# Expert tiles 7 to 17 of a GAT and mixture-of-experts kernel: rows loaded as 32 by 32 blocks and turned by VectorE

## The chip, the core and the metric

The kernel runs on one core of a Trainium2 chip. The metric is the device time of one launch in microseconds; lower is better. The engines are TensorE (PE, with its weight loads shown apart as PEld), VectorE (DVE), ScalarE (ACT), GpSimd (POOL) and SyncE (SP, which here only issues DMAs).

## What is computed

One layer has two halves. The first is a graph attention over 4096 nodes of 256 features with 4 heads of 64 and a dense 4096 by 4096 adjacency matrix. The second is a mixture of 8 experts with hidden size 1024, of which every node uses two.

```python
def _L0_ffn_ref(x, Wg, bg, W1, b1, W2, b2):
    xf = x.reshape(-1, D)
    gate_logits = xf @ Wg + bg
    top_w, top_i = jax.lax.top_k(gate_logits, TOP_K)
    top_w = jax.nn.softmax(top_w, axis=-1)
    w_dense = jnp.sum(jax.nn.one_hot(top_i, E, dtype=xf.dtype) * top_w[..., None], axis=1)
    out = jnp.zeros_like(xf)
    for e in range(E):
        h = jax.nn.gelu(xf @ W1[e] + b1[e], approximate=False)
        out = out + w_dense[:, e:e + 1] * (h @ W2[e] + b2[e])
    return out.reshape(B, L, D)

x = x + _L0_gnn_ref(_layernorm(x, axis=-1), adj, ...)
x = x + _L0_ffn_ref((_layernorm(x, axis=-1))[None], ...)[0]
```

All of it is in float32. The change touches the second half only.

## The kernel before

**The attention half** walks over the rows of the result in four blocks of 1024 and, for each, over 32 tiles of 128 neighbours. VectorE makes the weights of a tile (L1686), TensorE sums rows and denominators with them (L1195, L1204). While a block of rows is summed, the block before it is finished, normalised and routed: each row's two experts are found, and POOL writes the row (256 values and four numbers: two weights, the row's number and its first expert) to both experts' lists in HBM with indirect DMAs (L1382, tensor `lists`). So the lists fill block by block.

**The expert half** begins at about 778 us of the profile. It goes over tiles of an expert's list, in an order that is written out in `todo`: nine tiles `early` and eight tiles `mid`, each of 256 rows that are known to be full once the first three blocks have been routed; then eight tiles `final`, one for the rest of each list, of 288 to 512 rows (`FINAL`); then two tiles `rest` of 256 rows. Counted from 0, tiles 0 to 16 are the seventeen full ones. The first tile's rows and its first weights are loaded while the attention still runs. The last block of rows is finished and routed in pieces (`between`) beside tiles 0 to 5.

For each tile i the loop at the end of `forward` does, in this order of the program:

- `fetch` of tile i+1, all DMAs of SP's one queue: the expert's second bias (`b2b`, L1786), its first weights (`w1`, 1 MB, issued in `load_first`, L597) and its second weights (`w2`, 1 MB, L1793). `w1`, `w2` and `b2b` have two buffers each, so `w1` of a tile waits until TensorE has done the first product of two tiles before, `w2` until it has done the second, and `b2b` until ScalarE has scaled it (`b2s`, L1889).
- `up`: the first product, `ph`, 32 matmuls of 256 columns for a full tile (L1867), with a gelu by ScalarE of each of the eight results (L1871).
- `turn` of tile i+1: `prepare` makes the bias, the row numbers and the shares on VectorE (L1805 to L1835), and then the rows, which the experts' products need with features on partitions, are turned.
- `down`: the second product, `po`, again 32 matmuls of 256 columns for a full tile (L1901), in two halves of 128 rows. VectorE scales each half into `o` (L1914, nine buffers), and POOL adds it to the output with an indirect DMA (L1926).

On TensorE the order of a tile is thus up(i), the transposes of tile i+1, down(i). That order is kept by `queue` and `order_of` while the last block is being routed.

**Rows are loaded and turned in two ways.** For the seventeen full tiles `load_rows_of` (L554) loads 256 rows of 1040 bytes with one DMA into a buffer `early` (`ROOM` = 10 buffers): ten tiles ahead of the loop, and one more in each turn of the loop until all are loaded. `turn_rows_of` (L600) then transposes them on TensorE, 2 x 2 squares of 128 by 128 against the identity (L604), and ScalarE (L606) or VectorE (L608) copies the two results from PSUM to `xT`. For `final` and `rest` tiles `load_blocks_of` (L575) issues nine DMAs: one for the four numbers of each row (`known`, L580) and eight (two halves of the features by four quarters of the partitions, L587), each of which puts runs of 32 floats so that every 32 by 32 block stands where its transpose has to be. One VectorE instruction turns all blocks (`nc.vector.transpose`, L1851). `xr`, `known` and `xT` have two buffers each.

Loads of tiles behind the tenth (`late`) wait only for list entries that the third block wrote, not for those of the last block; loads of `final` and `rest` tiles wait for all of them, and for POOL's writes of zeros behind the lists' ends (L507).

Each SP DMA uses the next of eight completion semaphores, and before SP issues one it waits until the DMA eight places before it has landed.

Of the kernel before, what the change touches and what calls it, by code (L numbers as in the profile page):

```python
# [10 lines left out]
F32 = mybir.dt.float32  # L11
# [18 lines left out]
CH = P  # L30
TT = 2 * CH
WT = 4 * CH
FINAL = (16, 15, 15, 15, 13, 13, 12, 9)
LIST = 36 * CH
# [10 lines left out]
def gat_then_moe(  # L45
# [19 lines left out]
    nc = tc.nc  # L65
    N, D = x.shape
    H, _, K = W.shape
    E, _, F = W1.shape
# [10 lines left out]
    EARLY, BOTH = (-(-(2 * (N - k * R) - E * (TT - 1)) // TT) for k in (2, 1))  # L79
    MID = BOTH - EARLY  # L80
    LATE = 2 * N // TT - BOTH
    SURE = 2
    ROOM = 10
    KT = -(-N // TT)
    LAG = 6

# [1 line left out]
    W_1, W_2, ID, FIRST, RW = D, D + 1, D + 2, D + 3, D + 4  # L88
# [18 lines left out]
    lists = nc.dram_tensor("lists", [E * LIST, RW], F32, kind="Internal").ap()  # L107
# [111 lines left out]
    def forward(apart, stack):  # L219
# [49 lines left out]
        def tables(tag, width):  # L269

            return {
                "expert": moe_tile(f"expert{tag}", [P, width]),
                "mark": moe_tile(f"mark{tag}", [P, width]),
                "own": moe_tile(f"own{tag}", [P, width, E]),
                "place": moe_tile(f"place{tag}", [P, width]),
                "rows": moe_tile(f"rows{tag}", [P, width]),
                "float": moe_tile(f"float{tag}", [P, 2, width]),
                "int": moe_tile(f"int{tag}", [P, 2, width], I32),
                "past": moe_tile(f"past{tag}", [P, width, E]),
                "upto": moe_tile(f"upto{tag}", [P, E]),  # L280
            }
# [61 lines left out]
        early, mid, rest, final, over = tables("e", EARLY), {}, {}, {}, {}  # L343
# [174 lines left out]
        listed, earlier = [], []  # L518

        def after(ins, other, reason):  # L520
            tc.add_manual_dep(
                ins, other.name,
                mybir.DependencyInfo(mybir.DependencyClass.Sync, mybir.DependencyReason.DATA),
                reason=reason,
            )
# [25 lines left out]
        def entry(t, row, i, top):  # L551
            return nc.values_load(
                t["int"][0:1, row, i : i + 1], engines=[mybir.EngineType.SP],
                min_val=0, max_val=top, skip_runtime_bounds_check_because=why,  # L554
            )

        def load_rows_of(t, i, xr, late=False):
            rows = TT
            first = entry(t, 1, i, E * LIST - WT)
            ins = nc.sync.dma_start(  # L560
                xr, lists[bass.ds(first, rows), :].rearrange("(c p) d -> p c d", p=CH)
            ).ins
            if late:
                for i in earlier:
                    after(ins, i, "rows of the tile")
                for i in listed + clearing:
                    tc.declare_no_dep(ins, i.name, reason="rows behind those of the tile")
            else:
                for i in listed:
                    after(ins, i, "rows of the tile")  # L570

        def rows_of_job(t, i):
            return FINAL[i] * Q if t is final else TT

        def load_blocks_of(t, i, xb, known):  # L575


            first = entry(t, 1, i, E * LIST - WT)
            n = known.shape[1] * CH
            begun = [nc.sync.dma_start(  # L580
                known, lists[bass.ds(first, n), D:].rearrange("(c p) d -> p c d", p=CH)
            )]
            rows = lists[bass.ds(first, rows_of_job(t, i)), :]
            for c in range(DC):
                for a in range(P // Q):
                    here = c * P + a * Q
                    begun.append(nc.sync.dma_start(  # L587
                        xb[ts(a, Q), c], rows[:, here : here + Q].rearrange("(k p) d -> p k d", p=Q)
                    ))
            for ins in begun:  # L590
                for i in listed:
                    after(ins.ins, i, "rows of the tile")

        def load_first(t, i, w1):

            e = entry(t, 0, i, E - 1)
            nc.sync.dma_start(w1, W1[bass.ds(e, 1)].rearrange("o (c p) f -> p (o c) f", p=P))  # L597


        def turn_rows_of(xr, xT):  # L600
            for c in range(DC):
                pt = bank([P, TT], "pt")
                for k in range(TT // CH):
                    order_of(nc.tensor.transpose(pt[:, ts(k, CH)], xr[:, k, ts(c, P)], ident))  # L604
                if c % 2 == 0 or strict[0] or (ordered[0] and given_out):
                    nc.scalar.copy(xT[:, c, :], pt)  # L606
                else:
                    nc.vector.tensor_copy(xT[:, c, :], pt)  # L608
# [3 lines left out]
        with ExitStack() as layer:  # L612
# [964 lines left out]
            def first_tile():  # L1577

                load_rows_of(early, 0, xr0)
                load_first(early, 0, w10)  # L1580
# [26 lines left out]
            if not apart:  # L1607

                with tc.tile_pool(name="gen", bufs=2) as work:
# [12 lines left out]
                    for b in range(NB):  # L1622
                        mine = range(b * B, (b + 1) * B)
                        rows, top = er0[:, 0], er0[:, 1]
# [136 lines left out]
        work = ffn.enter_context(tc.tile_pool(name="ffn", bufs=2))  # L1761

        full_rows = [xr0]
# [9 lines left out]
        def fetch(t, i):  # L1773

            rows = rows_of_job(t, i)
            nch = -(-rows // CH)
            if t is early or t is mid:
                xr = full_rows[i + EARLY * (t is mid)]
                known = xr[:, :, D:]
            else:  # L1780
                xr = work.tile([P, DC, rows // Q, Q], F32, tag="xr", name="xr")
                known = work.tile([CH, nch, RW - D], F32, tag="known", name="known")
                load_blocks_of(t, i, xr, known)
            e = entry(t, 0, i, E - 1)
            b2b = work.tile([CH, D], F32, tag="b2b", name="b2b")
            nc.sync.dma_start(b2b, b2[bass.ds(e, 1)].to_broadcast([CH, D]))  # L1786
            if t is early and i == 0:
                w1 = w10
            else:
                w1 = work.tile([P, DC, F], F32, tag="w1", name="w1")  # L1790
                load_first(t, i, w1)
            w2 = work.tile([P, FC, D], F32, tag="w2", name="w2")
            nc.sync.dma_start(w2, W2[bass.ds(e, 1)].rearrange("o (c p) d -> p (o c) d", p=P))  # L1793
            job = {"t": t, "i": i, "xr": xr, "known": known, "w1": w1, "w2": w2, "nch": nch, "b2b": b2b}
            job["rows"] = rows
            job["last"] = t is rest and i == SURE - 1

            job["into"] = out[: N - R] if t is early or t is mid else out
            return job
# [38 lines left out]
        def turn(job):  # L1838
            xr = job["xr"]
            if given_out:  # L1840
                with tc.issue_after(given_out[-1]):
                    prepare(job)
            else:
                prepare(job)
            if job["t"] is early and job["i"] == 0:
                return xT0
            xT = work.tile([P, DC, job["rows"]], F32, tag="xT", name="xT")
            if job["t"] is early or job["t"] is mid:
                turn_rows_of(xr, xT)
            else:  # L1850
                nc.vector.transpose(  # L1851
                    xT.rearrange("p c i -> p (c i)"), xr.rearrange("p c k q -> p (c k q)")
                )
            return xT
# [134 lines left out]
        given = []  # L1989

        def load_full(i):
            xr = work.tile([CH, 2, RW], F32, tag="early", name="early", bufs=ROOM)
            load_rows_of(*((early, i) if i < EARLY else (mid, i - EARLY)), xr, i > ROOM)
            full_rows.append(xr)

        for i in range(1, ROOM + 1):
            load_full(i)
            if i in (1, 4):
                jobs.append(fetch(*todo[len(jobs)]))
            if i in (1, 2):  # L2000
                given.append(loads_of(b0 + i - 1, (residuals, large)[i - 1]))
        job = jobs[0]
        xT = turn(job)
        for i in range(len(todo)):
            if i + 1 == len(jobs) and i + 1 < len(todo):
                jobs.append(fetch(*todo[i + 1]))
            nxt = jobs[i + 1] if i + 1 < len(todo) else None
            if i and len(full_rows) < BOTH:
                load_full(len(full_rows))
            hT = up(job, xT)  # L2010
            between(2 * i)
            if nxt:
                xT = turn(nxt)
            giving = down(job, hT)
            next(giving)
            if nxt:
                next(giving, None)
            between(2 * i + 1)
            if tails:
                tails.pop(0)()  # L2020
            job = nxt
# [84 lines left out]
```

## Time and profile before

| what | value |
|---|---|
| median of 3 runs (1264.42 to 1270.94) | 1264.79 us |
| the profiled execution's own time | 1259.9 us |
| its span, first to last instruction | 1258.2 us |
| mean granted TensorE clock | 0.997 |
| PE / DVE / ACT / POOL busy | 1243.7 / 842.8 / 451.6 / 240.2 us |
| PE matmul of a tile's first product (L1867) | 864 of them, mean 423 ns |
| PE transposes of expert tiles (L604) | 68 of 128x128, median 273 ns |
| VectorE transposes of 128x512 (L1851) | 2, mean 711 ns |
| SP row loads (early<-lists) | 16 of 260 KB |
| SP block loads (xr<-lists) of 256 rows | 16 of 32 KB |

Busy times are sums of an engine's instruction records. Matmuls are pipelined: a record lasts longer than the distance from one matmul to the next, so the path is read from the chain of waits, which gives start, length and number of instructions of each piece. Window views give for a stretch of the span the length, then the busy time and number of instructions of PE, PEld, DVE, ACT and POOL, then the granted clock, the mean busy share of the 16 DMA engines (it can pass 1 in a short window) and the GB/s. A timeline row gives start, length, engine, line and operation; a bracket gives the idle time before it and what ended that.

### The profile page before, as it was taken

The numbers are of one execution on the slowest core, as the hardware profiler recorded it, in microseconds if no ns is written. First come the engines' busy times: TensorE is split into PE (matmuls) and PEld (weight loads), VectorE is DVE, ScalarE is ACT, GpSimd is POOL, SyncE is SP. The second block draws the span as 40 slices with busy tenths as digits, with TensorE's granted clock in tenths as the row PEclk, the third lists the DMA queues.
The fourth block names the chain that finished last, engine by engine and source line by source line (L and its number), as shares of the span: only waits on it lengthen the run. The fifth ranks groups of instructions, "written<-read, shape, count | busy, mean of one in ns | idle before, by whom it ended". The sixth has DMA issues, their size and how long they took to land.

```text
span 1258.2 us, 22490 instructions
## 1 busy us (share of the span) xinstructions
PE 1243.7 (99%) x8916; PEld 650.9 (52%) x8916; DVE 842.8 (67%) x1566; ACT 451.6 (36%) x929; POOL 240.2 (19%) x217
## 2 busy tenths in 40 slices
PE   9999999999999999999999999999999999999997
PEld 5444444332232332332325324888888876666686
DVE  7998887879999989999999996845111121111120
ACT  4332322255522375322655322533333332222322
POOL 4000000001002601006110024135222322122222
PEclk9999999999999999999999999999999999999999
DMA  6333433436533656335366423967777795454662
GB/s 215 118 119 124 158 105 102 166 102 133 187 105 104 231 118 201 103 100 158 112 167 194 119 80 108 329 184 225 234 208 222 207 210 115 102 139 105 139 156 42
DMA packets 131603, 190.22 MB, mean 151 GB/s; under 512 B 45560, under 2 KB 101744, under 8 KB 131104
## 3 DMA queue, kind: packets, MB, share of 16 engines
q1 hardware_dynamic: 109456, 145.39, 38.7%
q0 software_dynamic: 20544, 36.74, 13.2%
q10 hardware_dynamic: 1488, 6.55, 1.4%
q8 instruction: 72, 1.18, 0.4%
q14 instruction: 43, 0.35, 0.1%
HBM read 155.77 MB, written 29.74 MB: 147 GB/s over the span
## 4 chain that ended last, share of the span: by engine, by line
PE 94%; DVE 3%; issue 1%; DMA 1%; ACT 1%; POOLq 0%; SPq 0%; DVEq 0%; ACTq 0%
PE acc L1195 33%; PE po L1901 18%; PE ph L1867 17%; PE den L1204 17%; PE pr L1050 2%; DVE w L1686 2%; PE ph L1098 2%; PE pt L604 1%; PE ptx L1250 0%; DMA early<-lists 0%; PE acc L891 0%; PE pt L777 0%; PE ptr L1488 0%; PE po L1940 0%; PE pl L1261 0%
## 5 line engine op out<-in xcount | busy, mean ns | idle before, releaser
L1195 PE MATMUL acc<-w,ha 128*32 128x512 f32 x4096 | 671.6, 595 | 1.3 <-ACT u L1398 0.9
L1686 DVE SCALAR_TENSOR_TENSOR w<-er,eb,am 128x1024 f32<-128x1024 f32 x496 | 606.1, 1277 | 32.1 <-PE den L1204 31.8
L1204 PE MATMUL den<-w,unit 128*2 128x512 f32 x2048 | 467.8, 593 | 0.1
L1195 PEld LDWEIGHTS acc<-w,ha 128*32 128x32 f32 x4096 | 184.7, 110 | 294.3 <-issue 255.5
L1603 ACT ACTIVATE am<-adj 128x1024 bf16<-128x1024 int32 x124 | 130.6, 1054 | 348.8 <-DVE w L1686 208.9
L1867 PE MATMUL ph<-xT,w 128*128 128x256 f32 (+5 forms) x864 | 229.9, 423 | 0.2 <-ACT hT L1871 0.2
L1901 PE MATMUL po<-w,hT 128*128 128x256 f32 (+1 forms) x1040 | 229.7, 379 | 0.0
L1871 ACT ACTIVATE hT<-ph,bias 128x256 f32<-128x256 f32 (+5 forms) x216 | 111.3, 517 | 289.7 <-PE ph L1867 175.4
L1901 PEld LDWEIGHTS po<-w,hT 128*128 128x128 f32 (+1 forms) x1040 | 194.8, 189 | 30.7 <-issue 3.4
L1867 PEld LDWEIGHTS ph<-xT,w 128*128 128x128 f32 x864 | 163.4, 190 | 59.7 <-issue 38.0
L1204 PEld LDWEIGHTS den<-w,unit 128*2 128x2 f32 x2048 | 93.7, 85 | 148.2 <-issue 139.8
L1926 POOL DMA_INDIRECT out<-o,ids x66 | 102.0, 1546 | 323.7 <-DMA out<-o,ids 126.9
L1914 DVE SCALAR_TENSOR_TENSOR o<-po,share,b2s 128x256 f32<-128x256 f32 (+2 forms) x66 | 31.8, 483 | 196.4 <-PE po L1901 188.3
L1382 POOL DMA_INDIRECT lists<-xe,at x64 | 88.1, 1377 | 267.3 <-issue 184.3
L608 DVE COPY xT<-pt 128x256 f32<-128x256 f32 x12 | 5.1, 424 | 62.0 <-PE pt L604 54.1
L1851 DVE STREAM_TRANSPOSE xT<-xr 128x960 f32<-128x960 f32 (+5 forms) x10 | 10.0, 1004 | 31.6 <-PE ph L1867 31.1
L1050 PE MATMUL pr<-wr,xT 128*128 128x256 f32 x128 | 30.4, 381 | 0.2 <-ACT er L1144 0.2
L1889 ACT ACTIVATE b2s<-b2b,share 128x256 f32<-128x256 f32 x68 | 30.3, 503 | 0.0
L1438 POOL DMA_DIRECT2D xf<-in_x x6 | 8.1, 1351 | 105.4 <-ACT xf L1437 105.4
L1118 POOL DMA_DIRECT2D residual<-rb x6 | 4.7, 784 | 121.2 <-DVE rb L1065 121.2
L1050 PEld LDWEIGHTS pr<-wr,xT 128*128 128x128 f32 x128 | 24.1, 190 | 5.4 <-issue 0.9
L1098 PE MATMUL ph<-wall,xT 128*128 128x264 f32 x96 | 24.6, 399 | 0.0
(391 smaller groups left out, 658.5 us busy)
## 6 DMA issues: line engine op xcount, KB each, us to landing
adj<-in_adj SPq DMA_DIRECT2D x126, 512.0 KB
w<-in_L_ffn_W SPq DMA_DIRECT2D x54, 1024.0 KB
er<-parts ACTq DMA_DIRECT2D x3, 2048.0 KB
early<-lists SPq DMA_DIRECT2D x16, 260.0 KB
lists<-zeros POOLq DMA_DIRECT2D x8, 520.0 KB
residual<-rb POOLq DMA_DIRECT2D x8, 512.0 KB
rb<-residual SPq DMA_DIRECT2D x8, 512.0 KB
out<-y POOLq DMA_DIRECT2D x8, 512.0 KB
```

The costliest lines, as they stand in the source:

```text
L1050: order_of(nc.tensor.matmul(pr[:, k, :], turned[b][:, c, ts(t0 + k, P)], wr[:, c, :], start=(c == 0), stop=(c == DC - 1),))
L1098: order_of(nc.tensor.matmul(phs[t - t0], xT[:, c, ts(t, P)], wall[:, c, :], start=(c == 0), stop=(c == DC - 1),))
L1195: queue(nc.tensor.matmul(acc[half][h // 2][here : here + Q, :], ha[:, j, h * K + g * Q : h * K + (g + 1) * Q], w[half][h], start=(j == 0), ...
L1204: queue(nc.tensor.matmul(den[here : here + HB, :], unit[:, j, h, 1 - half : 1 - half + HB], w[half][h], start=(j == 0 and half == 0), stop ...
L1382: ins = nc.gpsimd.indirect_dma_start(lists, bass.IndirectOffsetOnAxis(ap=at[:, k, t : t + 1], axis=0), xe[:, t, :], None,).ins
L1603: nc.scalar.activation(am, at, AF.Relu, scale=2.0)
L1686: marks["w"] = nc.vector.scalar_tensor_tensor(wh[:, these], er[:, these, h], eb[:, j, h : h + 1], mask[:, these], op0=OP.max, op1=OP.min,).ins
L1867: order_of(nc.tensor.matmul(ph, job["w1"][:, c, ts(f, P)], xT[:, c, :], start=(c == 0), stop=(c == DC - 1),))
L1871: job["gelu"] = nc.scalar.activation(hT[:, f, :], ph, AF.Gelu, bias=job["bias"][:, f : f + 1]).ins
L1901: order_of(nc.tensor.matmul(po[:size], hT[:, f, k * CH : k * CH + size], w2[:, f, :], start=(f == 0), stop=(f == FC - 1),))
L1914: given_out.append(nc.vector.scalar_tensor_tensor(o[:size], po[:size], share[:size, k : k + 1], b2s[k][:size], op0=OP.mult, op1=OP.add,).ins)
L1926: added.append(add().ins)
```

## The change

Of the seventeen full tiles only the first six (0 to 5) keep row loads and TensorE transposes; five `early` buffers, all filled ahead of the loop, serve tiles 1 to 5. Tiles 6 to 16 (the seventh to the seventeenth) are loaded inside `fetch` by `load_blocks_of`, one tile ahead of the loop as `final` tiles are, and turned by VectorE. The rule of what such a load waits for (`late`) is taken into `needs_of` and kept for them; tiles 6 to 10, which were among the ten loaded ahead, now have it too. The call in the loop that loaded one further tile's rows is gone.

```diff
-    ROOM = 10
+    NEAR = 6
...
-        def load_rows_of(t, i, xr, late=False):
-            rows = TT
-            first = entry(t, 1, i, E * LIST - WT)
-            ins = nc.sync.dma_start(
-                xr, lists[bass.ds(first, rows), :].rearrange("(c p) d -> p c d", p=CH)
-            ).ins
+        def needs_of(ins, late):
+
             if late:
                 for i in earlier:
                     after(ins, i, "rows of the tile")
...
-        def load_blocks_of(t, i, xb, known):
+        def load_blocks_of(t, i, xb, known, late):
...
             for ins in begun:
-                for i in listed:
-                    after(ins.ins, i, "rows of the tile")
+                needs_of(ins.ins, late)
...
-            if t is early or t is mid:
-                xr = full_rows[i + EARLY * (t is mid)]
+            chosen = t is early or t is mid
+            near = chosen and i + EARLY * (t is mid) < NEAR
+            if near:
+                xr = full_rows[i]
                 known = xr[:, :, D:]
             else:
                 xr = work.tile([P, DC, rows // Q, Q], F32, tag="xr", name="xr")
                 known = work.tile([CH, nch, RW - D], F32, tag="known", name="known")
-                load_blocks_of(t, i, xr, known)
+                load_blocks_of(t, i, xr, known, chosen)
...
-            if job["t"] is early or job["t"] is mid:
+            if job["near"]:
                 turn_rows_of(xr, xT)
             else:
                 nc.vector.transpose(
...
         def load_full(i):
-            xr = work.tile([CH, 2, RW], F32, tag="early", name="early", bufs=ROOM)
-            load_rows_of(*((early, i) if i < EARLY else (mid, i - EARLY)), xr, i > ROOM)
+            xr = work.tile([CH, 2, RW], F32, tag="early", name="early", bufs=NEAR - 1)
+            load_rows_of(early, i, xr)
             full_rows.append(xr)
 
-        for i in range(1, ROOM + 1):
+        for i in range(1, NEAR):
             load_full(i)
...
-            if i and len(full_rows) < BOTH:
-                load_full(len(full_rows))
```

More of the change, by code (lines that the diff above doesn't have):

```diff
@@ L570, in load_rows_of @@
                     after(ins, i, "rows of the tile")
+        def load_rows_of(t, i, xr):
+            rows = TT
+            first = entry(t, 1, i, E * LIST - WT)
+            ins = nc.sync.dma_start(
+                xr, lists[bass.ds(first, rows), :].rearrange("(c p) d -> p c d", p=CH)
+            ).ins
+            needs_of(ins, False)
         def rows_of_job(t, i):
             return FINAL[i] * Q if t is final else TT
-        def load_blocks_of(t, i, xb, known):
+        def load_blocks_of(t, i, xb, known, late):
             first = entry(t, 1, i, E * LIST - WT)
@@ L1794, in fetch @@
             job = {"t": t, "i": i, "xr": xr, "known": known, "w1": w1, "w2": w2, "nch": nch, "b2b": b2b}
-            job["rows"] = rows
+            job["rows"], job["near"] = rows, near
             job["last"] = t is rest and i == SURE - 1
```

## The prediction

> **What bounds the kernel now.** I read the page's chain first: it says which engine sets the end.
>
> ```profile
> PE 94%; DVE 3%; issue 1%; DMA 1%; ACT 1%; POOLq 0%; SPq 0%; DVEq 0%; ACTq 0%
> ```
>
> TensorE holds 94% of the path. The change touches only the expert half, so next I read that half's chain in order of time, around the last full tiles (start, length, piece).
>
> ```profile
> 980.47 0.44 PE pt L604 x4
> 980.91 6.91 PE po L1901 x32
> 987.82 6.91 PE ph L1867 x32
> 994.72 0.44 PE pt L604 x4
> 995.16 6.91 PE po L1901 x32
> 1002.07 6.91 PE ph L1867 x32
> 1008.98 0.44 PE pt L604 x4
> 1009.41 6.91 PE po L1901 x32
> 1016.32 6.91 PE ph L1867 x32
> 1023.23 6.91 PE po L1901 x32
> 1030.13 5.15 PE ph L1867 x12
> ```
>
> Pieces follow each other without a gap. A full tile takes 1002.07 - 987.82 = 14.25 us: two products of 6.91 and 0.44 of transposes. Tile 16, from 1016.32, has no transposes behind its `ph` in the program before, since the tile after it already comes in blocks: 1030.13 - 1016.32 = 13.81 us. So the state after the change is already there for one tile, and TensorE closes the gap at once. Third, the windows by tile, to see what else is near its limit (columns as in the table's text; the last two are DMA share and GB/s).
>
> ```profile
> 888.00:902.30 14.30, 14.30 (x70) 12.60 (x69) 2.14 (x9) 4.85 (x11) 3.79 (x4) 1.00 0.86 251
> 902.30:916.50 14.20, 14.20 (x70) 12.50 (x69) 2.15 (x9) 4.85 (x11) 3.97 (x4) 1.00 0.87 234
> 987.80:1002.00 14.20, 14.20 (x70) 12.50 (x69) 2.15 (x9) 4.85 (x11) 4.08 (x3) 1.00 0.70 180
> 1002.00:1016.30 14.30, 14.30 (x70) 12.60 (x69) 2.15 (x9) 4.85 (x11) 3.10 (x2) 1.00 0.93 205
> 1016.30:1030.10 13.80, 13.80 (x66) 12.15 (x65) 3.11 (x10) 4.58 (x10) 3.10 (x2) 1.00 0.88 180
> ```
>
> VectorE works 2.15 us of 14.2 and ScalarE 4.85: both have room. The DMA engines are the second resource, at 0.70 to 0.87, and at 0.93 and 0.88 where blocks are loaded beside a full tile (the last two rows).
>
> **What the Trainium skill says.** (1) "TensorE: Matmul & The Clock Gate", Part 4: PE-mode transpose: a transpose is a matmul against the identity, its result lands in PSUM and needs a copy; about 275 ns for one in a kernel. The trace has 273 ns as median at L604, but four, pipelined, take 0.44 us of the path, and that is what counts. (2) "VectorE: DVE Perf Modes", The three transpose paths: VectorE turns only 32 by 32 blocks. That is why the DMA must place the blocks; the trace has it at L1851 (711 ns for 128x512). (3) "DMA: Bandwidth & Descriptors", Specifications: full rate needs pieces of 512 B or more. Block loads move runs of 128 B, row loads 1040 B. The trace agrees in kind: see the DMA cost below. (4) The same page, Issuing engines are not separate DMA queues: SP's and POOL's DMAs share the same engines, so blocks compete with weights and with the sums added to the output. The share of 0.93 fits.
>
> **The change, part by part.**
>
> *Removed: TensorE transposes.* In the built program TensorE's list lacks eleven rows of four transposes and is otherwise in the same order. The chain has them at 866.45 to 1008.98, each 0.44 us (14.25 - 13.81), all on the path: 11 x 0.44 = 4.8 us.
>
> *Removed: copies to `xT`.* 22 copies of about 0.36 us (ScalarE) or 0.42 (VectorE). ScalarE's idle time before gelus is a wait for `ph`, so they lie beside TensorE's work: 0.
>
> *Added: VectorE's transposes.* 11 x 0.71 = 7.8 us on VectorE, which idles 12 of 14 us. In the built list the transpose for tile t stands two tiles ahead, in the second product of tile t-2, behind that tile's first `o`. Let T be the start of `up` of tile t-2; it then runs at about T + 6.9 + 3.45 + 0.5 = T + 10.9, and its result is wanted at T + 27.6. Behind it in VectorE's queue stand the second `o` of that tile and the next `prepare`; TensorE wants that `o` read only when its bank is written again, at about T + 24. So a wait of up to 12 us here costs TensorE nothing.
>
> *Added: block loads.* SP's rows for tile 15's period, where the first blocks are loaded (512 rows, twice of ours):
>
> ```profile
> 1002.10 0.37 SPq L1793 DMA_DIRECT2D w<-in_L_ffn_W  x1
> 1003.27 0.37 SPq L580 DMA_DIRECT2D known<-lists  x1
> 1003.84 6.26 SPq L587 DMA_DIRECT2D xr<-lists  x8
> 1010.67 0.36 SPq L1786 DMA_DIRECT2D b2b<-in_L_ffn_b  x1
> ```
>
> The nine DMAs go out between the `w2` at T and the `b2b` at T + 8.6. In periods without blocks SP sits waiting there (b2b at 982.07, 8.5 us after T = 973.56; 996.32 is the same), since `b2b` needs ScalarE's buffer. So SP's eleven times eight further issues hide in that wait. Blocks of 256 rows for the `rest` tiles took SP 5.41 us (1187.56) and 5.72 (1207.60). Part of that is the ring of eight semaphores: the seventh block waits for `w2` to land. They should land by T + 11, about when VectorE asks; 12 us of tolerance stand behind. If this cover were gone, each microsecond beyond would be paid once per tile, 11 us per microsecond.
>
> *DMA time, the cost that no row gives.* Times are share x length. A quiet window has 0.70 x 14.2 = 9.9 us. The two with blocks have 13.3 and 12.1; their surplus over two quiet ones is 5.6 us for 512 + 480 rows, 1.4 us for 256. Bound from above: all of the first window's surplus (13.3 - 9.9 = 3.4) is charged to 256 rows, if fixed cost per DMA rules. From below: tiles 6 to 9 lose their row load in the loop, so the net can be 0 or slightly negative there. I take 1.4. The eight windows from 888 to 1002 average 0.777 x 14.25 = 11.1 us; with 1.4 it is 12.5 of the 13.81 that remain, 0.90. The worst, 0.87 x 14.2 = 12.4, comes to 13.8, just full. Weights have a lead: `w1` is issued at T + 9.7 (983.30) and needed at T + 27.6; with about 8 us in flight (the estimate from the seventh block's wait) 10 us remain, so a few full windows cost nothing. Cost: 0.
>
> *POOL's queue.* No POOL instruction moves. Its sums are already late by 12 to 21 us (tile 11's second `o` at 959.4, its add at 976.00), and slower adds would lengthen that; nine `o` buffers allow about 60 us. The list ends are cleared at 976.98 at the latest, and the first `final` load that waits for this is due at 1003.27 - 4.8. Cost: 0, cover 20 us.
>
> *Fewer row loads at the opening.* Five loads of 260 KB (and the loop's six) go. SP issued seven in a row at 796.98 to 803.64, with the DMA share near 1. TensorE idles 2.1 us in 780 to 845 (62.89 busy of 65), but what ends these gaps is ScalarE and VectorE (0.6, 0.5, 0.3, 0.2), and the one row load in the chain, 5.91 us at 780.59, is tile 1's, issued before. So 0; at most 2.1 us gained.
>
> *Sum.* -4.8 us. The profiled execution took 1259.9 (span 1258.2), so 1255.1 for its like. The median of the three runs is 1264.79, 4.9 above the profiled execution; I subtract the same amount there: **1260.0 us**, 0.38% less.
>
> **Rivals.**
>
> *A, forecast: the transposes' time is simply gone.* For: tile 16 at 13.81. 1260.0, with a spread of 1.5.
>
> *B: weights become late and eat part of the gain.* If DMA time per tile is D, the lag over 11 tiles is 11 x (D - 13.81), less 10 us of lead. The gain is gone at D = 15.2, where 11 x 1.35 = 14.8. For D of 14.7 to 15.2 the time is 1260 to 1265. For it: shares of 0.93 and more in short windows. Against: the mean D is 12.5.
>
> *C, slower: the DMA engines become the bound.* Same mechanism, past its point: D = 15.2. With the upper bound everywhere, the worst window's 12.4 plus 3.4 = 15.8 for all eleven tiles, the lag is 21.9 - 10 = 11.9 us, and with -4.8 the time is 1264.8 + 7.1 = 1271.9. TensorE would show gaps ended by `w`. Against: half of the windows before have 10 us, not 12.4.
>
> *D: the opening gains too.* With fewer rows in the crowded stretch the 2.1 us of gaps close: 1264.8 - 6.9 = 1257.9. Against: their releasers are engines.
>
> *E: the gap is filled by another engine.* If gelu or the copy chain held TensorE, removing transposes would gain nothing, 1264.8. Eight gelus of 0.47 take 3.8 of 6.91 us, and tile 16 speaks against it: counted in B.
>
> **How the numbers follow.** A 0.72, B with E 0.13, C 0.08, D 0.07. About 0.5% (6.3 us) is what a measurement of this kernel can tell from no change, so faster is below 1258.5 and slower above 1271.1. A lies inside, but for its lower edge (0.05); D is faster, B inside, C slower: faster 0.12, same 0.80, slower 0.08. For eight in ten, the range takes in A, most of B and most of D: 1257.2 to 1265.2. It leaves out C and the edges.
>
> **What would show it.** Right: the chain has pairs of 6.91 and 6.91 with no `pt` after that of tile 5 (851.99 before), a full tile takes 13.81 us from 866 on, and the first `final` product starts 4.8 us earlier against 1030.13. VectorE's transposes of 128x512 are 13, near 0.71 us; DMA shares in those windows are 0.85 to 1. Wrong: a gap on TensorE before `ph` or `po` that ends with `w` (B, C), a transpose by VectorE that waits past T + 23, or a different start of the expert half. The forecast fails if D exceeds 15 us.

## The result, and the profile after

The kernel after takes 1260.59 us (median of 8 runs, 1259.27 to 1266.17), the kernel before in the same comparison 1265.8 us (8 runs). The ratio is 0.996, with a 95% interval of 0.9942 to 0.9979. A second comparison of the same two kernels gave 1254.9 against 1259.94 us, ratio 0.9964 (0.9952 to 0.9977). Both kernels lie nearly 6 us lower there than in the first comparison, so only ratios of one comparison are used below; 0.0036 of 1260 is 4.5 us. Forecast were 4.8 us less and 1260.0 us.

The profiled execution of after took 1260.56 us, its span is 1258.8 us against 1258.2 before. The two single profiles thus hide the gain, and the chain tells why. First the page's shares of the chain in after:

```profile
PE 93%; DVE 3%; issue 1%; ACT 1%; DMA 1%; POOLq 0%; SPq 0%; DVEq 0%; ACTq 0%
```

TensorE still sets the end. The chain of after in order of time (start, length, piece) around the last full tiles:

```profile
1003.07 6.91 PE ph L1872 x32
1009.98 6.91 PE po L1906 x32
1016.88 6.91 PE ph L1872 x32
1023.79 6.91 PE po L1906 x32
1030.70 13.73 PE ph L1872 x32
```

No `pt` is left: a tile takes 1016.88 - 1003.07 = 13.81 us where it took 14.25. The same chain earlier, where the first tiles in blocks are loaded:

```profile
869.68 6.91 PE po L1906 x32
876.59 6.04 PE ph L1872 x28
882.63 1.90 issue
884.53 1.13 PE ph L1872 x4
885.66 6.91 PE po L1906 x32
892.57 6.91 PE ph L1872 x32
```

Here is something the forecast had not: TensorE stands still for 1.90 us in the middle of `ph`. And the rest of the difference lies ahead of the change. The last of VectorE's 528 `w` instructions in the attention half starts at 771.49 us in after, at 767.11 before; the 513th starts at 746.99 and 748.44. So this chain lost about 6 us between 747 and 771 in after, in code that the change does not touch. None of the twelve later profiles has this loss (their last `w` starts between 765.4 and 768.8). It belongs to that one execution, and its cause is not shown. What the profile does show is where it falls: into a row of sixteen scatters that GpSimd issues into the lists (745.5 to 770.4 us), where ready instructions start late. ScalarE's copy of transposes that TensorE had done at 768.2 starts at 772.4:

```profile
772.37 0.65 ACT L609 COPY xT<-pt 128x256 f32<-128x256 f32 x2 [19.37 <-remote]
```

Before has the same row of scatters at 746.9 to 773.1 without such a loss. I therefore measure the expert half from the end of TensorE's last `den`, with which the attention ends on the chain, to the end of the span:

| profiled execution | last `den` ends | end | expert half | TensorE idle from 850 to 890 |
|---|---|---|---|---|
| before | 778.69 | 1258.2 | 479.5 | none over 0.1 |
| after | 781.98 | 1258.8 | 476.8 | 1.90 |
| after, second comparison | 777.00 | 1253.1 | 476.1 | 0.60 |
| after, list scatters spread (below) | 778.81 | 1253.6 | 474.8 | none over 0.1 |

Without an idle piece the half is 479.5 - 474.8 = 4.7 us shorter. In the two profiles of after it is 2.7 and 3.4 us shorter; with their idle pieces taken off, 4.6 and 4.0.

The tile windows of after (the sum's columns as before; the last two are DMA share and GB/s) answer to those of before:

```profile
902.40:916.20 13.80, 13.80 (x66) 12.15 (x65) 2.43 (x9) 4.58 (x10) 4.50 (x4) 1.00 0.95 246
916.20:930.00 13.80, 13.80 (x66) 12.15 (x65) 2.34 (x9) 4.58 (x10) 4.14 (x4) 1.00 0.93 241
930.00:943.80 13.80, 13.80 (x66) 12.15 (x65) 2.34 (x9) 4.58 (x10) 3.23 (x4) 1.00 0.92 237
943.80:957.60 13.80, 13.80 (x66) 12.15 (x65) 2.43 (x9) 4.58 (x10) 4.26 (x4) 1.00 0.93 241
957.60:971.40 13.80, 13.80 (x66) 12.15 (x65) 2.34 (x9) 4.58 (x10) 3.24 (x4) 1.00 0.91 238
971.40:985.20 13.80, 13.80 (x65) 12.16 (x64) 2.43 (x9) 4.58 (x10) 3.34 (x4) 1.00 0.86 237
985.20:999.00 13.80, 13.80 (x65) 12.16 (x64) 2.38 (x9) 4.58 (x10) 4.41 (x3) 1.00 0.83 205
```

The mean share is 0.904, or 12.5 us per tile of 13.81. The same seven windows of before (not shown; shares 0.87, 0.83, 0.72, 0.73, 0.69, 0.78 and 0.70) have 0.760, or 10.8 us per tile of 14.25. In the second profile of after they have 0.929, or 12.8 us. TensorE is busy throughout in every row shown.

VectorE's new transposes in after, as a group (count, then busy us, mean ns, idle before):

```profile
L1856 DVE STREAM_TRANSPOSE xT<-xr 128x512 f32<-128x512 f32 x13 | 9.2, 709 | 10.6 <-PE ph L1872 8.3 <-DMA b2b<-in_L_ffn_b 1.7 <-issue 0.5
```

One of them in VectorE's timeline, in the tile whose `up` starts at T = 934.0:

```profile
944.46 0.48 DVE L1919 SCALAR_TENSOR_TENSOR o<-po,share,b2s 128x256 f32<-128x256 f32 x1 [9.09 <-PE po L1906]
945.85 0.71 DVE L1856 STREAM_TRANSPOSE xT<-xr 128x512 f32<-128x512 f32 x1 [0.91 <-DMA b2b<-in_L_ffn_b]
947.91 0.48 DVE L1919 SCALAR_TENSOR_TENSOR o<-po,share,b2s 128x256 f32<-128x256 f32 x1 [1.35 <-PE po L1906]
```

It runs at T + 11.8 after a wait of 0.91 us for a DMA, and VectorE is idle again before the next `o`. SP's queue for the tile after it:

```profile
947.85 0.38 SPq L1798 DMA_DIRECT2D w<-in_L_ffn_W  x1
948.82 0.37 SPq L584 DMA_DIRECT2D known<-lists  x1
949.42 5.58 SPq L591 DMA_DIRECT2D xr<-lists  x8
956.05 0.36 SPq L1791 DMA_DIRECT2D b2b<-in_L_ffn_b  x1
```

With T = 947.8 the nine DMAs leave between T + 1 and T + 7.2, and `b2b` at T + 8.2, as early as before (T + 8.5).

### The profile page after: what moved, and what is told of

It is laid out like the page before. It is cut to its first block, busy times and chain, and to the rows that moved or that the text cites. A ratio compares the mean times of both kernels' runs of the same rounds, so it can differ in the third digit from the quotient of the medians.

```text
span 1258.8 us, 22720 instructions
## 1 busy us (share of the span) xinstructions
PE 1241.7 (99%) x8872; PEld 650.4 (52%) x8872; DVE 845.5 (67%) x1566; ACT 448.3 (36%) x918; POOL 240.4 (19%) x217
## 4 chain that ended last, share of the span: by engine, by line
PE 93%; DVE 3%; issue 1%; ACT 1%; DMA 1%; POOLq 0%; SPq 0%; DVEq 0%; ACTq 0%
PE acc L1198 33%; PE po L1906 18%; PE ph L1872 17%; PE den L1207 17%; PE pr L1053 2%; DVE w L1689 2%; PE ph L1101 2%; PE ptx L1253 0%; DMA early<-lists 0%; PE acc L894 0%; PE pt L780 0%; PE ptr L1491 0%; PE po L1945 0%; PE pl L1264 0%; PE po L875 0%
## 5 line engine op out<-in xcount | busy, mean ns | idle before, releaser
L1856 DVE STREAM_TRANSPOSE xT<-xr 128x512 f32<-128x512 f32 (+5 forms) x21 | 17.8, 850 | 34.0 <-PE ph L1872 31.2
L207 ACT ACTIVATE m<-y,off 128x256 f32<-128x256 f32 x48 | 23.7, 495 | 1.1 <-DVE off L215 0.6
```

## The experiments

Each text names its theories itself. The numbers 2 and 3 stand for other theories in the first four texts than in the later eight, which were formed after the first results. "Before" is the kernel before, timed in the same comparison.

**After, unchanged.** No edit. It gives the level, and shows which gaps come back.

> The changed kernel unchanged, for a second profile and a paired time. Theory 1 (only the 44 TensorE transposes count, 4.8 us): ratio to the kernel before 0.996; the profile again has 13.81 us per full tile. Theory 4 (the two TensorE gaps of 5.8 and 1.9 us in the first profile, near 767 and 883 us, that nothing in the profile releases, belong to the change): they are there again at the same places. If they are chance, they stand elsewhere or are missing, and the span is shorter by what is missing, down to about 1251.

Measured: ratio 0.9964 (0.9952 to 0.9977). The idle piece is 0.60 us in this profile, again at 881 us, and the loss near 767 is absent. (The text's 5.8 us there is VectorE's loss; TensorE reached its last `den` about 4.7 us late, with no single idle piece over 0.9.) The gain is real; the gap is of changing size but lies in the same stretch.

**Turned by VectorE, loaded as before.**

```diff
-            if job["t"] is early or job["t"] is mid:
+            if (job["t"] is early or job["t"] is mid) and job["i"] + EARLY * (job["t"] is mid) >= 6:
+                for k in range(2):
+                    nc.vector.transpose(xT[:, k, :], xr[:, k, :D])
+            elif job["t"] is early or job["t"] is mid:
```

> The kernel before with TensorE's transposes of tiles 6 to 16 left out: VectorE turns the row buffers within 32 by 32 squares instead (two instructions of 128x256 per tile, so that these tiles' rows reach the experts in a wrong arrangement), and no block is loaded. It has the part of the change that takes work from TensorE and no other. Theory 1: 0.996, the same as the changed kernel. Theory 3 (block loads take back part of a larger gain): clearly below the changed kernel, 0.994 or less. Theory 2 (part of the change's gain comes from fewer row loads at the opening): above it, 0.997 to 0.998.

Measured: ratio 0.9948 (0.993 to 0.9965), 4.4 to 8.8 us less. It covers the 4.8 us of the removed transposes. Its interval overlaps that of after, so whether the loads take back part of a larger gain (theory 3) is not decided. No block of a full tile is loaded here, and yet TensorE has an idle piece in the same stretch, longer than either of after's:

```profile
877.46 6.00 PE L1870 MATMUL ph<-xT,w 128*128 128x256 f32 x20 [3.03 <-ACT hT L1874]
```

So the added loads are not needed for such a piece. The profiled execution is the slowest of the five, 4.5 us over their median, which suggests that the piece is not in every execution.

**Block loads and VectorE's transposes beside everything else.**

```diff
+                if i + EARLY * (t is mid) >= 6:
+                    xs = work.tile([P, DC, rows // Q, Q], F32, tag="xr", name="xr")
+                    ks = work.tile([CH, nch, RW - D], F32, tag="known", name="known")
+                    load_blocks_of(t, i, xs, ks, True)
...
+                    nc.vector.transpose(
+                        sT.rearrange("p c i -> p (c i)"), xs.rearrange("p c k q -> p (c k q)")
+                    )
```

> The kernel before with all its row loads and TensorE transposes, and with the block loads and VectorE transposes of tiles 6 to 16 added into spare buffers that nobody reads. It pays all that the change adds and saves nothing. Theory 1: 1.000, within 0.1%. Theory 3 (blocks cost time through the DMA engines): above 1.001, with gaps on TensorE before ph or po. In its DMA shares the stretch 888 to 1002 rises from 0.78 by 1.4 us per tile of 14.25, to 0.88.

Measured: ratio 1.0022 (1.0011 to 1.0033), 2.8 us more. So what the change adds is not free. The DMA share rose as expected, from 0.78 in before (first row) to 0.88 (second), which is 1.4 us per tile:

```profile
888.00:1002.00 114.00, 114.00 (x546) 100.39 (x545) 17.16 (x72) 38.80 (x88) 31.14 (x25) 1.00 0.78 221
888.00:1002.00 114.00, 114.00 (x546) 100.39 (x545) 22.49 (x80) 38.80 (x88) 29.30 (x23) 1.00 0.88 227
```

TensorE is busy throughout in both rows. All but 0.2 us of TensorE's additional idle time lies in one place, at 876 to 881 us. ScalarE's timeline of this kernel there:

```profile
873.74 0.47 ACT L1890 ACTIVATE hT<-ph,bias 128x256 f32<-128x256 f32 x1 [6.81 <-PE ph L1886]
877.26 0.47 ACT L1890 ACTIVATE hT<-ph,bias 128x256 f32<-128x256 f32 x1 [3.06 <-PE ph L1886]
880.13 1.20 ACT L1890 ACTIVATE hT<-ph,bias 128x256 f32<-128x256 f32 x3 [2.39 <-PE ph L1886]
```

The gelus should follow each other by 0.86 us, one per four matmuls. Here the second comes 3.5 us after the first, though its `ph` was long done, and TensorE, which has three banks for `ph`, waits for ScalarE to free one, as its chain shows:

```profile
872.69 4.55 PE ph L1886 x16
877.24 0.02 issue
877.26 0.48 ACT hT L1890
877.75 0.04 issue
877.79 2.31 PE ph L1886 x4
880.11 0.02 issue
880.13 0.48 ACT hT L1890
```

Before has late gelus at the same time. They cost TensorE nothing there; the lateness is smaller than what three banks cover:

```profile
876.42 0.47 ACT L1871 ACTIVATE hT<-ph,bias 128x256 f32<-128x256 f32 x1 [0.39 <-issue]
877.29 0.47 ACT L1871 ACTIVATE hT<-ph,bias 128x256 f32<-128x256 f32 x1 [0.39 <-PE ph L1867]
878.62 0.47 ACT L1871 ACTIVATE hT<-ph,bias 128x256 f32<-128x256 f32 x1 [0.86 <-PE ph L1867]
880.06 0.47 ACT L1871 ACTIVATE hT<-ph,bias 128x256 f32<-128x256 f32 x1 [0.97 <-PE ph L1867]
881.49 0.47 ACT L1871 ACTIVATE hT<-ph,bias 128x256 f32<-128x256 f32 x1 [0.95 <-PE pt L604]
```

At this time GpSimd issues the last block's eight scatters into the lists, one each 1.28 us (868.7 to 878.7 in the kernel with blocks beside, 871.6 to 881.5 in before). That became theory 3 of the later texts.

**Five early row buffers alone.** `ROOM = 5` in before.

> The kernel before with five row buffers in place of ten: five fewer row loads ahead of the loop, each of these issued later in the loop; everything else as before. Theory 1: 1.000. Theory 2 (the crowded opening gains): 0.9985 or less, up to 2.1 us of TensorE gaps gone between 780 and 845.

Measured: ratio 0.9995 (0.9986 to 1.0005). Fewer row loads ahead of the expert half gain nothing that shows; the 2.1 us of theory 2 lie outside of the interval.

**The loads alone beside.** The edit with blocks beside, without its transposes.

> The kernel before, with the block loads of tiles 6 to 16 issued in addition, into spare buffers that nothing reads: no VectorE transposes are added, TensorE's transposes and all row loads stay. This is the previous run of loads and transposes beside (1.0022, 2.8 us) without its VectorE part. Theory 1 (block loads cost nothing): 1.000. Theory 2 (the loads' transfers cost about 0.25 us per tile, 2.8 us in all): 1.002, with TensorE gaps. Theory 3 (the cost arises only in the crowded stretch of 868 to 885 us, where the last list scatters run): 1.001 to 1.002, with all extra gaps of TensorE inside that stretch. If the cost came from VectorE instead: 1.000.

Measured: ratio 1.0011 (0.9997 to 1.0025); idle pieces of 1.32 and 1.72 us at 878 and 881, none elsewhere in the tiles 6 to 16. The ratio alone decides between none of the theories; the place of the pieces is theory 3's.

**VectorE's transposes alone beside.**

```diff
+                if job["i"] + EARLY * (job["t"] is mid) >= 6:
+                    sT = work.tile([P, DC, job["rows"]], F32, tag="sT", name="sT", bufs=1)
+                    for k in range(2):
+                        nc.vector.transpose(sT[:, k, :], xr[:, k, :D])
```

> The kernel before, with VectorE transposes of tiles 6 to 16 in addition (two of 128x256 from the row buffer of the tile, into a spare buffer that nothing reads): no block loads, TensorE's transposes stay. Theories 1, 2 and 3: 1.000, VectorE has room. Rival (VectorE's added 0.7 us per tile delays the copies and output steps that TensorE needs): 1.002, 0.25 us per tile, with TensorE gaps that end with VectorE.

Measured: ratio 1.002 (1.0011 to 1.0029). Every theory but the rival expected 1.000. Yet the idle pieces are not one per tile, as the rival has it: there are two, 0.31 us at 864 and 1.84 us at 879, both ended by ScalarE. The run is not the test that it was meant to be, though. The rows of these tiles are loaded early, and in the trace the transposes run early too (count, then shortest, median and longest in ns, first and last start):

```profile
L1853 DVE STREAM_TRANSPOSE sT<-early x22: 402/436/446, 808.0 to 888.3; 128x256 f32<-128x256 f32 x22
```

Fourteen of the 22 had started by 828 us, 20 by 875, and some held up VectorE's list by waiting for a row load, for 5.17 us at most. So no price per tile could show here; the rival had to wait for the run with spread scatters, where one transpose per tile is there. What the run does show is that the same stretch is disturbed with no block loaded. This spoke for theory 3.

**Only tiles 11 to 16 by blocks.** `NEAR = 11` in after, where `load_full` loads rows of tiles 9 and 10 too. `fetch` still takes `full_rows[i]` for these two, the rows of tiles 0 and 1 (TensorE transposes from `early` 36 times, not 40): they compute with the wrong rows, in the same amount of work.

> The kernel after with only tiles 11 to 16 loaded in blocks (six tiles; ten early row buffers as before): no block load falls in the stretch of 868 to 885 us. Six tiles lose 0.44 us of TensorE's transposes. Theory 1: 2.6 us less than before, 0.998. Theory 2 (0.25 us per tile for the loads): 6 x 0.19 = 1.1 us less, 0.999. Theory 3: 2.6 us less, 0.998, with the stretch 868 to 885 as in the kernel before.

Measured: ratio 0.998 (0.9966 to 0.9994), 2.5 us less where 2.6 was expected, idle pieces of 0.42 and 0.30 us at 878 and 879, though no block load falls there and before has none. The interval also holds theory 2's 1.1 us.

**Tiles 3 to 16 by blocks.** `NEAR = 3` in after, with the tile fetched at `i in (1, 2)`.

> The kernel after with tiles 3 to 16 loaded in blocks (fourteen tiles, two early row buffers). Three more tiles lose 0.44 us of TensorE's transposes. Theory 1: 14 x 0.44 = 6.2 us less than before, 0.995. Theory 2: 14 x 0.19 = 2.7 us less, 0.998. Theory 3: what the kernel after gains (4.5) and 1.3 us more, 5.8 us less, 0.9954; the loads of tiles 3 to 5 fall at the start of the expert half, where weights are ahead.

Measured: ratio 0.9962 (0.9948 to 0.9976), no better than after; the numbers of theories 1 and 3 lie inside the interval as well. Its profile has an idle piece of 3.44 us at 873, followed by 3.41 us of half-speed clock.

**The scatters in groups of four, in after.**

```diff
+            for _ in range(2):
+                if held_lists:
+                    held_lists.pop(0)()
...
-                        ins = nc.gpsimd.indirect_dma_start(
-                            lists, bass.IndirectOffsetOnAxis(ap=at[:, k, t : t + 1], axis=0),
-                            xe[:, t, :], None,
-                        ).ins
...
+                        if ordered[0]:
+                            held_lists.append(partial(scatter, at, xe, k, t))
```

Clearing of the list ends starts after the last group, so tiles 14 and 15 clear a second one each. The edit thus moves GpSimd's sums and clearings as well as the scatters.

> The kernel after with the last block's list scatters on GpSimd issued four at a time, with sums into the output between them, where after issues eight in a row (868 to 884 us). Nothing else of note moves. Theory 3 (TensorE's extra gaps arise while eight scatters in a row run, since ScalarE and VectorE then react late): no gap of TensorE above 0.3 us from 850 to 900 us, no half-speed clock there, ratio to before 0.9955 to 0.996, at most 1 us under after. Theory 2 (the block loads' transfers cost time anywhere): as after, 0.9964, gaps as before. If the gaps have another cause than the scatters: gaps of 0.6 to 3 us stay in that stretch.

Measured: ratio 0.9964 (0.9952 to 0.9977). By the ratio alone theory 2's number came out. What speaks for theory 3 is the profile: the gap is gone, and the expert half is 4.7 us shorter than before, as the table shows. The 0.6 us that the gap cost in after's second profile are below what six runs can tell. The times also lie closer together: 1254.89 to 1255.24 us, where after's fourteen in the second comparison go from 1254.11 to 1259.78.

**The scatters in groups of four, with blocks and transposes beside.** The same edit in that kernel.

> The kernel before with block loads and VectorE transposes of tiles 6 to 16 into unread buffers in addition (TensorE's transposes stay), and the list scatters issued four at a time. With eight in a row this gave 1.0022. Theory 3 (loads and VectorE transposes are free outside the crowded stretch): 1.000 to 1.0005, gaps at 876 to 880 us gone. Theory 2: 1.0022 again, since loads and transposes are all there.

Measured: ratio 0.9998 (0.999 to 1.0006), where eight scatters in a row gave 1.0022 (1.0011 to 1.0033). This is the experiment that decides: all loads and all transposes of the change are there, one of VectorE's per tile, TensorE's transposes too, and the cost is gone. So theory 2 falls, and with it the rival of a price per transpose on VectorE. The expert half is 1258.3 - 778.62 = 479.7 us, 479.5 in before. The two kernels ran on two chips, each beside before, whose medians there are 1259.84 and 1259.94 us. Before with only its scatters spread was not run, so a gain of the spreading itself could hide in this ratio; but before has no idle piece over 0.1 us in the stretch that it could remove. The 14 times lie within 2.1 us, the 22 with eight scatters in a row within 7.2. ScalarE in this kernel during the second and third group:

```profile
889.80 0.47 ACT L1897 ACTIVATE hT<-ph,bias 128x256 f32<-128x256 f32 x1 [0.33 <-PE ph L1893]
890.67 0.47 ACT L1897 ACTIVATE hT<-ph,bias 128x256 f32<-128x256 f32 x1 [0.39 <-PE ph L1893]
891.53 0.47 ACT L1897 ACTIVATE hT<-ph,bias 128x256 f32<-128x256 f32 x1 [0.39 <-PE ph L1893]
892.39 0.47 ACT L1897 ACTIVATE hT<-ph,bias 128x256 f32<-128x256 f32 x1 [0.39 <-PE ph L1893]
```

The gelus are 0.86 us apart again.

**Both: tiles 3 to 16 by blocks, scatters in groups of four.**

> The kernel after with tiles 3 to 16 loaded in blocks and the list scatters issued four at a time. Without it the same fourteen tiles gave 0.9962, with a gap of 3.44 us and a half-speed clock at 873 to 881 us. Theory 1 with theory 3: 14 x 0.44 = 6.2 us less than before, 0.995, the gap gone; the best version so far. Theory 2: as near3, 0.9962.

Measured: ratio 0.9943 (0.9929 to 0.9956), 1252.71 against 1259.84 us, 7.1 us less. It is the best version run, and its interval lies nearly whole below that of after. The chain of this kernel shows where most of the part beyond 14 x 0.44 = 6.2 us comes from:

```profile
811.80 6.91 PE ph L1879 x32
818.71 0.87 PE ptx L1254 x8
819.58 6.91 PE po L1913 x32
```

In before TensorE waited 0.35 us at 819.9 and 0.24 us at 836.5, ahead of `pt`, for two of ScalarE's pieces (`b2s` and `xT`) to end. With tiles 3 to 5 in blocks these `pt` and their waits are gone.

**Three times the short runs.**

```diff
+            if late:
+                for n in range(2):
+                    more = work.tile([CH, 2, D // Q, Q + 1], F32, tag=f"more{n}", name=f"more{n}", bufs=2)
+                    for c in range(2):
+                        begun.append(nc.sync.dma_start(
+                            more[:, c, :, :Q],
+                            rows[c * CH : (c + 1) * CH, :D].rearrange("p (b q) -> p b q", q=Q),
+                        ))
```

> The kernel after with the rows of each tile 6 to 16 read twice more in runs of 128 B, by four further DMAs per tile into buffers that nothing reads: three times the short runs, at about 3 us more of SP's issuing. By the prediction's price (1.4 us of the DMA engines per 256 rows) a tile then needs 12.5 + 2.8 = 15.3 us of the DMA engines against 13.81: 1.5 us behind in each of eleven tiles, 16 in all, 10 of it covered by the weights' lead: 6 us slower than after, ratio to before 1.001. If a tile's short runs take 0.5 us or less, nothing changes: 0.9964. By the upper bound (3.4 us) 20 us and more slower than after: 1.02.

Measured: ratio 1.0173 (1.0154 to 1.0191), some 26 us slower than after. The waits of TensorE from 862 to 1060 us (us in total, times, longest):

```profile
PE ph L1880 <- DMA w<-in_L_ffn_W: 17.3, 7, 4.5
PE ph L1880 <- DVE xT L1864: 2.4, 1, 2.4
```

The weights come late: the sign that rival C named is there. The cost is four times the 6 us that my price gave. Two things were missing in it. With the 12.5 to 12.8 us per tile of after and 1.7 to 2.0 us for each set of runs (worked out below), an estimate for a tile is 15.9 to 16.8 us; 2.1 to 3.0 us behind in eleven tiles, less the 10 us of lead, make 13 to 23 us. The idle pieces from 900 us on sum to 19.7 us. And some of the pieces were followed by half-speed clock, 17.1 us in all, which cost another 8.5 us. What SP's four further issues per tile do to this was not separated from the transfers, and SP's queue is late too: it is a tile behind by 911 us, where `w2` leaves 0.62 us after `w1` (911.66 and 912.28; in after 4.4 us, at 943.47 and 947.85, as it waits for TensorE) and `w1` leaves only 4.6 us before TensorE wants it. So the run shows late weights, not that the DMA engines alone are the bound.

## Why the prediction was right, point by point

The absolute time, 1260.59 us against 1260.0, agrees better than it had to. In the second comparison after took 1254.9 us, below the forecast's range of 1257.2 to 1265.2, since both kernels lay lower. That the level stayed where the first three runs had it was luck; the difference of 4.8 us is what the forecast had right.

- **TensorE's transposes, 4.8 us on the path: right.** 13.81 us per tile, no `pt` after 855 us, and 4.7 us in the expert half of the profile without a gap. Leaving them out without any block load (turned by VectorE, loaded as before) gave 4.4 to 8.8 us.
- **Copies to `xT`, 0: right**, as far as the runs tell. No idle piece of TensorE in tiles 6 to 16 arose from their absence.
- **VectorE's transposes, hidden: right outside the stretch of the last scatters.** They take 709 ns each (0.71 forecast) and run at up to T + 11.8 (T + 10.9 forecast); two of the ten from 888 to 1030 us waited for a load, 0.91 us at the longest.
- **SP's nine DMAs hide in its wait before `b2b`: right.** `b2b` leaves at T + 8.2.
- **DMA time per tile: at the low end.** I took 1.4 us for 256 rows in blocks, with bounds of 0 and 3.4. With loads and transposes beside it came out at 1.4 (a share of 0.88 instead of 0.78), but at 2.0 with the scatters spread there (0.92). The seven windows of before and after give 12.5 - 10.8 = 1.7 us, and 2.0 in the second profile. The mean that I forecast, 12.5 us of 13.81, came out in the first profile all the same, since my base of 11.1 us took in one window more, from 888 to 902 us, with a higher share. The cost stayed 0, with about 1 us of room per tile; three times the short runs show what lies behind that.
- **POOL's queue, 0: right.** From 876 to 1020 us the sums follow their `o` by 8.5 to 20.4 us in after, by 6.1 to 20.8 us in before, well under the 60 us that nine buffers allow.
- **The opening, 0: right.** Five row buffers alone gave 0.9995; rival D falls.
- **What the forecast did not have:** "Cost: 0" for loads and transposes is wrong in the stretch of the last scatters. I checked the windows and the waits tile by tile, but not what ScalarE's gelus looked like in before at 877 to 883 us. There they were already 1.43 us apart instead of 0.86, a sign that TensorE's cover of three banks was being used up. In after this cost 1.90 and 0.60 us in two profiles. It is about what separates the 4.8 us of the sum from the 4.5 us measured, though the intervals are too wide to show that difference.

That spreading the scatters, with what it moves on GpSimd's queue, removes the cost of loads and transposes beside is shown (1.0022 to 0.9998). That the lateness needs the added loads is not: it is there in before, and 3.03 us of idle time came without any block of a full tile. Beside eight scatters in a row loads and transposes make it cost more (1.0022). Why ScalarE is late is not shown. An equal row of eight scatters at 848.5 to 858.4 us in before leaves the gelus 0.86 us apart; so does the row at 869.9 to 879.8 us in three times the short runs, in the very place and with a DMA share of 0.94 to 0.97; and in the spread kernel the DMA share reaches 1.14 (892 to 897 us) without a late gelu. So neither eight in a row nor full DMA engines alone do it.

## What to carry to other kernels

A tile that already does without a piece of work can show the gain of removing it from all, as long as the same engine stays the limit; here the tile without transposes gave 13.81 us, and every tile reached it. Where the added work is "hidden", look for the stretch where the hiding engines are already late though nothing waits yet: even spacing of an engine's instructions was a better sign of room here than its busy share. Look into the trace of an experiment for where the added work really ran; in VectorE's transposes alone beside nearly all of it ran ahead of the stretch in question. And compare profiles from a mark ahead of the change, taken on the engine that sets the end, since one execution can lose more elsewhere than the change brings.

## What the runs showed of the hardware that I had not expected

- ScalarE and VectorE start ready instructions late in the stretch of the second eight scatters, in ten of the eleven profiles of kernels that issue them so, and in none of the three that issue them in groups of four. (The exception is three times the short runs.) Gelus are 1.3 to 3.9 us apart instead of 0.86, or the first of a tile is 3 us late or more; VectorE starts up to 1.21 us after its own last result (879.80 us, VectorE's transposes alone beside). In after's first profile the like shows in the sixteen scatters before 770 us. Such lateness is named after `ph`, "issue" or "remote", whose work was done.
- Idle pieces of TensorE of 2.4 us or more, in one part or in two parts 1.1 us apart (2.41, 2.57, 3.03, 3.44, 3.95, 1.32 + 1.72, 1.65 + 1.73), each came with 3.41 us at half the clock that began within 1 us of their end, which costs 1.7 us more; with a piece of 4.45 us it was 6.83, from 1.8 us ahead of its end. Single pieces of 1.84, 1.90 and 2.09 us had none.
- A half-speed stretch of 3.41 us (once 6.83) also stands near 258 us or in the first 12 us of some executions, whatever the kernel. Such an event is worth as much as a third of this change.
